# First attention of a four-layer network: weighing one unit later, six of eight norms inside its loop, and preparation of weights in single steps

## The chip, the cores and the metric

One core of one Trainium2 chip runs the kernel. Its engines are TensorE (PE, with the weight loads PEld shown apart), VectorE (DVE), ScalarE (ACT), GpSimd (POOL) and SyncE (SP, which here only issues DMAs). The metric is the time of one execution on the device in microseconds. The kernel before takes 2339.91 us, the median of three runs (2333.78 to 2342.82).

## The reference

Four layers in turn work on 8 sequences of 512 tokens with 128 features, all in float32. Each layer is a norm, an attention-like block, a gate, and a feed-forward block. The change touches the first attention, and weights that later layers use. What it computes on the normed input:

```python
def window_kv(t):
    pad = jnp.concatenate([jnp.zeros((B, H, W, hd), t.dtype), t], axis=2)
    prev = pad[:, :, :S].reshape(B, H, nb, W, hd)
    cur = t.reshape(B, H, nb, W, hd)
    return jnp.concatenate([prev, cur], axis=3)
kw = window_kv(k)
vw = window_kv(v)
scores = jnp.einsum('bhnqd,bhnkd->bhnqk', qb, kw) * scale
...
scores = jnp.where(valid, scores, NEG)
attn = jax.nn.softmax(scores, axis=-1)
out = jnp.einsum('bhnqk,bhnkd->bhnqd', attn, vw)
...
return out @ Wo.T + bo
```

with 16 heads of 8 features and windows of W = 64 tokens, each of which sees itself and the window before. The norm ahead of it is `(x - m) / sqrt(v + eps)` over the 128 features. The weights of the first feed-forward block come as integers and are decoded by `q / 7.5 - 1`, times a scale for each group of 16. The second layer mixes each token with the one before it, by weights per feature. The last layer needs some scalars per head (softplus and sigmoid of parameters).

## The kernel before, in words

`x` and `xn` (the normed input) lie in SBUF with features on the 128 partitions and all 4096 tokens along the row. A sequence ("batch" b) is one tile of 512 tokens.

**Order.** Most code calls the engines through a wrapper (`in_order`, L83), which keeps an engine's instructions in the order in which they are written; nearly every row of the profile therefore has line L83, and tile names tell the rows apart. What is called without the wrapper (constants, `l0_decode`, `l3_scalars`, loads) is placed by the scheduler where an engine's queue has room. The tile framework puts in all waits, also those for a buffer of a pool.

**Start** (`network`, L2781). SP issues eight loads of `x`, then those of the second and third layers' constants, then the first attention's weights `a0_w` (tile a_w) and `a0_b`, then the integers `f0_q` and their scales. `layer_norm` (L142) goes over all eight tiles: `centre` (four matmuls with the centring matrix, tile ps_c), `spread` (square on ACT, sum on DVE, power on POOL: sq, var, rstd), `scale` on DVE (row), `turn` (four transposes, ps_t), `keep` (copy to xn on ACT). `l0_decode` (L2691) turns the integers into weights on DVE. The constants of the third and second layers are filled; `fill` of the second layer (L738) issues the two big loads of the expert weights from ACT's queue and computes the mixing weights there (td, rest, wm). `l3_scalars` (L2730) is written behind the first layer but placed early by the scheduler.

**The attention** (`l0_attention`, L250) handles 64 units: unit u is half the heads of 128 tokens, eight units to a batch. `project` computes a batch's k, q and v in five steps; the first two write the four pieces of kb (the keys, masked by head group), alternately on DVE and ACT, out of one PSUM tile ps_k. `scores(u)` (PE: sc; DVE: scale and mask into e, then the row maximum mx; POOL: subtract) runs three units ahead, the exp on ACT two units ahead. `turned(u)` transposes the exponentials on PE (tp) and ACT copies them to SBUF (pt). `weigh(u)` multiplies them with the values (av). Every second unit closes a pair: `norm` divides on DVE (rec, o), `out_rows` transposes the result (tpo) and ACT adds the bias (ot). `finish` projects a batch out (ps_o). tp, tpo, ps_k, ps_q, ps_v, ps_o all take turns in one pool `p_t` of three PSUM buffers. The loop (L408) writes the parts of unit u in this order: `turned(u)`, `norm(u - 1)`, `scores(u + 3)`, `out_rows(u - 1)`, exp of u + 2, `weigh(u)`, `finish`, one step of `project`, and from the fifth batch on a step of `l0_low_rank`, which finishes the first feed-forward block's weights.

## Time and profile before

| what | value |
|---|---|
| median of three runs | 2339.91 us |
| the profiled execution: time, span | 2359.42 us, 2357.7 us |
| busy share of the span | PE 93%, DVE 85%, ACT 79%, POOL 67% |
| mean granted TensorE clock | 0.965 of full |
| first PE instruction of the attention (ps_k) | 29.09 us |
| first transposes of exponentials (tp) | 48.46 us |
| last output projection of the attention (ps_o) | from 311.94 us |

The profile is one execution. A row of the timeline has start, length, engine, line, operation, output and inputs, shape, count, and in brackets how long the engine had been idle before it and what ended that idle time. In the table of stretches each engine's busy time is followed by the number of its instructions, then come the granted clock, the share of time in which DMA engines were busy, and GB/s. A matmul in float32 shows as two passes, so four matmuls count x8; four transposes count x4.

### The profile page before, as it was taken

What the parts mean: (1) busy time and instruction counts of PE and PEld (TensorE: products, weight loads), DVE (VectorE), ACT (ScalarE), POOL (GpSimd) and SP (SyncE); (2) the same over time, 40 slices, a digit from 0 to 9 for tenths busy, and PEclk for the clock granted to TensorE, in tenths of its full rate; (3) what the DMA queues carried; (4) which work ended last, traced back from release to release, by engine and by line L of the source; (5) the groups of instructions that cost most, each with busy time, mean ns of one, the idle gap of its engine ahead of it and who ended that gap; (6) DMA issues with size and microseconds to landing.
All of it is one profiled execution on the core that took longest, in us unless ns stands there. A gap on an engine that the chain in (4) does not pass through costs nothing.

```text
span 2357.7 us, 48954 instructions
## 1 busy us (share of the span) xinstructions
PE 2186.5 (93%) x17762; PEld 1526.4 (65%) x17762; DVE 1996.3 (85%) x3579; ACT 1856.3 (79%) x3906; POOL 1576.9 (67%) x1414
## 2 busy tenths in 40 slices
PE   6999998899976999878999999999999999999888
PEld 4666676556523666645776777777777777777776
DVE  4777777985676999759999999999999999999656
ACT  4666664564533899848999999999999999999875
POOL 4444435355274788656788788887888878887554
PEclk7999988999997999989999999999999999999999
DMA  4000001013110000043443444334443344433100
GB/s 142 2 2 2 2 1 36 14 50 72 40 46 14 3 16 16 29 134 100 106 104 90 110 114 106 101 91 110 112 109 100 92 110 113 108 97 84 43 1 37
DMA packets 91617, 156.94 MB, mean 67 GB/s; under 512 B 20144, under 2 KB 44464, under 8 KB 91120
## 3 DMA queue, kind: packets, MB, share of 16 engines
q1 hardware_dynamic: 86736, 140.95, 22.9%
q0 software_dynamic: 4352, 8.92, 1.6%
q10 hardware_dynamic: 288, 3.93, 0.4%
q8 instruction: 142, 2.33, 0.4%
q14 instruction: 99, 0.81, 0.1%
HBM read 30.52 MB, written 12.06 MB: 18 GB/s over the span
## 4 chain that ended last, share of the span: by engine, by line
PE 56%; DVE 30%; issue 4%; ACT 4%; POOL 3%; DMA 1%; SPq 1%; another core or an unknown queue 0%; DVEq 0%; ACTq 0%; POOLq 0%
PE sc L83 10%; DVE sc L83 8%; DVE y L83 6%; DVE r L83 6%; PE ps_av L83 6%; PE ps_u L83 5%; PE tp L83 5%; PE ps_kq L83 4%; PE ps_ab L83 3%; PE av L83 3%; PE ps_n L83 2%; DVE mx L83 2%; DVE e L83 2%; PE ps_v L83 2%; PE ps_y L83 1%
## 5 line engine op out<-in xcount | busy, mean ns | idle before, releaser
L83 POOL TENSOR_TENSOR ek<-E,kn 128x512 f32<-128x512 f32 (+3 forms) x512 | 434.4, 871 | 206.3 <-DMA kn<-nr 205.1
L83 PE MATMUL sc<-r 128*128 128x512 f32 (+3 forms) x1024 | 310.2, 446 | 25.2 <-DVE y L83 22.2
L83 POOL TENSOR_TENSOR e<-e,mx 128x1024 f32<-128x1024 f32 x112 | 212.2, 1900 | 180.8 <-DVE mx L83 94.7
L83 POOL TENSOR_TENSOR r<-r,rs 128x1024 f32<-128x1024 f32 x128 | 304.4, 2378 | 23.0 <-DMA rs<-r 20.9
L83 PE MATMUL ps_av<-u,at 128*128 128x128 f32 x2560 | 307.9, 276 | 0.8 <-ACT o L83 0.8
L83 PEld LDWEIGHTS ps_av<-u,at 128*128 128x128 f32 x2560 | 297.3, 193 | 1.1 <-ACT o L83 1.1
L83 ACT ACTIVATE y<-y,mn 128x384 f32<-128x384 f32 (+3 forms) x512 | 288.6, 569 | 4.0 <-DVE mn L83 3.2
L83 PEld LDWEIGHTS sc<-r 128*128 128x128 f32 x1024 | 165.6, 192 | 190.0 <-issue 118.8
L83 DVE SCALAR_TENSOR_TENSOR y<-sc,qn,V 128x512 f32<-128x512 f32 (+3 forms) x512 | 246.5, 544 | 9.1 <-DVE sc L83 0.5
L83 DVE CUSTOM_DVE_ANT_0 y<-y,ps_g,ncs 128x384 f32<-128x384 f32 (+3 forms) x512 | 253.4, 541 | 0.0
L83 PEld LDWEIGHTS tp<-ident,y 128*128 128x128 f32 x1280 | 161.5, 141 | 115.3 <-issue 49.5
L83 ACT ACT_TABLE_LOAD x175 | 224.5, 1283 | 4.0 <-PEq L2879 0.8
L83 PE MATMUL tp<-ident,y 128*128 128x128 f32 x1280 | 203.9, 274 | 3.4 <-ACT o L83 1.4
L83 ACT COPY at<-tp 128x512 f32<-128x512 f32 (+1 forms) x384 | 195.2, 509 | 7.2 <-PE tp L83 4.4
L83 DVE TENSOR_TENSOR sc<-sc,EF 128x1280 f32<-128x1280 f32 x128 | 192.0, 1500 | 4.4
L83 DVE SCALAR_TENSOR_TENSOR sc<-sc,ek 128x1280 f32<-128x1280 f32 x128 | 189.8, 1483 | 6.5 <-issue 5.0
L83 POOL TENSOR_TENSOR s<-s,o 128x512 f32<-128x512 f32 x120 | 154.1, 1284 | 31.6 <-ACT o L83 31.6
L83 ACT ACTIVATE y<-y 128x1280 f32<-128x1280 f32 x128 | 163.4, 1277 | 5.1 <-DVE y L83 4.4
L83 DVE TENSOR_TENSOR r<-sn,ps_kq 128x1024 f32<-128x1024 f32 x128 | 155.3, 1213 | 9.6 <-ACT sq L83 5.1
L83 ACT ACTIVATE sq<-ps_kq 128x1024 f32<-128x1024 f32 x128 | 131.6, 1028 | 32.3 <-PE ps_kq L83 32.3
L83 DVE TENSOR_TENSOR r<-ct,ps_kq 128x1024 f32<-128x1024 f32 x128 | 155.3, 1213 | 0.0
L83 ACT ACTIVATE e<-e 128x1024 f32<-128x1024 f32 x112 | 117.3, 1062 | 40.9 <-POOL e L83 40.5
(465 smaller groups left out, 5023.3 us busy)
## 6 DMA issues: line engine op xcount, KB each, us to landing
rs<-r SPq DMA_DIRECT2D x256, 256.0 KB
kn<-nr SPq DMA_DIRECT2D x512, 64.0 KB
yrows<-yy SPq DMA_DIRECT2D x36, 128.0 KB
ct<-trig SPq DMA_DIRECT2D x16, 256.0 KB
EF<-E SPq DMA_DIRECT2D x16, 256.0 KB
EF<-E SPq DMA_DIRECT2D x16, 192.0 KB
m_w<-m_w ACTq DMA_DIRECT2D x1, 2560.0 KB
x<-x SPq DMA_DIRECT2D x8, 256.0 KB
```

What stands on the lines that cost most here:

```text
L83: ins = op(*args, **kwargs)
```

## The change

- **Norms.** `layer_norm` takes the number of tiles and does two. The other six are written into the attention's loop in five parts at fixed units: `centre` (PE to PSUM, copied to SBUF tile lc by ACT), `square` (ACT), `spread` (DVE sum, POOL power), `scale_rows` (four ACT scalings, where DVE had one multiply), `turn_rows` (PE transposes into p_t, ACT copy to xn). The norm of tile b has its centre in the last unit of batch b - 3 and its turn in unit 6 of batch b - 2; tile 2 is done within batch 0.
- **Weighing.** `weigh(u - 1)` stands where `weigh(u)` stood. `norm`, `out_rows` and `finish` are a unit later; a pair closes in odd units. pt moves to the pool with four buffers. The loop has one iteration more.
- **Preparation in steps.** `l0_decode`, the mixing weights and `l3_scalars` are generators, called in order at three units of each batch from the second on. The multiply with the scales moves from DVE to POOL; the load of the last layer's parameters is issued by SP behind all others.
- **Loads.** The second and third layers' constants are loaded behind the first layer's. The expert weights are loaded from SP's queue instead of ACT's.

The core of the diff:

```diff
-    def layer_norm(self, x, xn, gamma=None, beta=None, banks=(5, 3), free=False):
+    def layer_norm(self, x, xn, gamma=None, beta=None, banks=(5, 3), free=False, n=NTB):
...
-                pt = p3.tile([P, 4, P], F32, tag="pt", name="pt")
+                pt = p5.tile([P, 4, P], F32, tag="pt", name="pt")
...
+        mid, sqs, std = {}, {}, {}
+        def centre(b):
+            ps = p_t.tile([P, 4, P], F32, tag="t", name="ps_c")
+            for k in range(4):
+                pe.matmul(
+                    ps[:, k, :], lhsT=x[:, ts(4 * b + k, P)], rhs=net.cmat,
+                    start=True, stop=True,
+                )
+            mid[b] = p2.tile([P, 4, P], F32, tag="lc", name="lc")
+            act.copy(mid[b], ps)
+        def square(b):
+            sqs[b] = p2.tile([P, 4, P], F32, tag="sq", name="sq")
+            act.activation(sqs[b], mid[b], AF.Square, scale=net.inv_root)
+        def spread(b):
+            var = p2.tile([P, 4], F32, tag="var", name="var")
+            std[b] = p2.tile([P, 4], F32, tag="rstd", name="rstd")
+            dve.tensor_reduce(var, sqs.pop(b), AX.X, ALU.add)
+            dve.tensor_scalar(var, var, EPS, None, ALU.add)
+            pool.tensor_tensor(std[b], var, net.neg_half.to_broadcast([P, 4]), ALU.pow)
+        def scale_rows(b):
+            for k in range(4):
+                act.activation(
+                    mid[b][:, k, :], mid[b][:, k, :], AF.Copy, scale=std[b][:, k : k + 1]
+                )
+        def turn_rows(b):
+            ps = p_t.tile([P, 4, P], F32, tag="t", name="ps_t")
+            for k in range(4):
+                pe.transpose(ps[:, k, :], mid[b][:, k, :], net.ident)
+            act.copy(xn[:, ts(b, S)], ps.rearrange("p k q -> p (k q)"))
+        norms = {}
+        for b in range(2, B):
+            c = U * (b - 3) + 7 if b > 2 else 1
+            for part, at in (
+                (centre, c), (square, c + 1), (spread, c + 2), (scale_rows, c + 4),
+                (turn_rows, U * (b - 2) + 6),
+            ):
+                norms.setdefault(at, []).append((part, b))
+        def early():
+            yield from net.prep.l0_decode(dve, pool)
+            yield from l1.mixing(act)
+            yield from net.prep.l3_scalars(dve, act)
+        rest = early()
         todo = iter(())
-        for u in range(N + 2):
+        pts = {}
+        for u in range(N + 3):
...
-            ended = u >= 1 and u <= N and u % 2 == 0
+            ended = u >= 3 and u % 2 == 1
             if u < N:
-                pts = turned(u)
+                pts[u] = turned(u)
             if ended:
-                o = norm(u - 1)
+                o = norm(u - 2)
...
-            if u < N:
-                weigh(u, pts)
-            if u >= U and u % U == 1:
+            if 1 <= u <= N:
+                weigh(u - 1, pts.pop(u - 1))
+            if u >= U and u % U == 2:
                 finish(u // U - 1)
             next(todo, None)
+            for part, b in norms.get(u, ()):
+                part(b)
+            if u >= U and u % U in (1, 3, 6):
+                next(rest, None)
...
-            if u > 4 * U and u % U == 6:
+            if u > 4 * U and u % U == 5:
                 next(low, None)
...
-        self.w13 = net.load(p1, "m1_w13", act)
-        self.w2 = net.load(p1, "m1_w2", act)
+        self.w13 = net.load(p1, "m1_w13")
+        self.w2 = net.load(p1, "m1_w2")
...
-    def l0_decode(self):
-        nc, wt, qw, sc = self.net.nc, self.f0_wt, self.qw, self.sc
-        nc.vector.tensor_copy(wt, qw)
-        nc.vector.tensor_scalar(wt, wt, 1.0 / 7.5, -1.0, ALU.mult, ALU.add)
-        nc.vector.tensor_tensor(wt, wt, sc, ALU.mult)
+    def l0_decode(self, dve, pool):
+        wt, qw, sc = self.f0_wt, self.qw, self.sc
+        dve.tensor_copy(wt, qw)
+        yield
+        dve.tensor_scalar(wt, wt, 1.0 / 7.5, -1.0, ALU.mult, ALU.add)
+        yield
+        pool.tensor_tensor(wt, wt, sc, ALU.mult)
+        yield
...
-            net.layer_norm(x, xn)
-            prep.l0_decode()
+            l2.load()
+            l1.load()
+            net.layer_norm(x, xn, n=2)
             l2.fill()
             l1.fill()
-            l0_attention(net, xn, s, p0, w0, b0)
+            l0_attention(net, x, xn, s, p0, w0, b0, l1)
             l0_ffn(net, x, xn, s, l1)
-        prep.l3_scalars()
```

`l1.mixing` holds the instructions that computed td, rest, wm in `fill`, and `l3_scalars` the same instructions as before, both with a `yield` every few of them. The step of `l3_scalars` with the function Ln stands alone.

More of the change, by code (lines that the diff above doesn't have):

```diff
@@ L190, in keep @@
                     act.activation(xn[:, ts(t, TB)], ps, AF.Identity, scale=gamma, bias=beta)
-            for t in range(NTB + 3):
-                if t < NTB:
+            for t in range(n + 3):
+                if t < n:
                     centre(t)
                     spread(t)
-                if 2 <= t < NTB + 2:
+                if 2 <= t < n + 2:
                     scale(t - 2)
@@ L247, in window_mask, with l0_attention @@
             )
-def l0_attention(net, xn, s_out, p0, w, bias):
+def l0_attention(net, x, xn, s_out, p0, w, bias, l1):
     nc, tc = net.nc, net.tc
@@ L418, in l0_attention @@
             if ended:
-                out_rows(u - 1, o)
+                out_rows(u - 2, o)
             if u + 2 < N:
                 act.activation(e[u + 2], e[u + 2], AF.Exp)
-            if u < N:
-                weigh(u, pts)
-            if u >= U and u % U == 1:
+            if 1 <= u <= N:
+                weigh(u - 1, pts.pop(u - 1))
+            if u >= U and u % U == 2:
                 finish(u // U - 1)
             next(todo, None)
+            for part, b in norms.get(u, ()):
+                part(b)
+            if u >= U and u % U in (1, 3, 6):
+                next(rest, None)
             if u == 4 * U:
@@ L430, in l0_attention @@
                 )
-            if u > 4 * U and u % U == 6:
+            if u > 4 * U and u % U == 5:
                 next(low, None)
+        for _ in rest:
+            pass
 L0_FFN = (
@@ L729, in __init__, with load @@
         self.net = net
-        self.p1 = p1 = st.enter_context(tc.tile_pool(name="a1_c", bufs=1))
+        self.p1 = st.enter_context(tc.tile_pool(name="a1_c", bufs=1))
+    def load(self):
+        net, nc, p1, E = self.net, self.net.nc, self.p1, self.E
         self.rw = net.load(p1, "m1_r")
@@ L739, in fill @@
         net, nc, p1, E = self.net, self.net.nc, self.p1, self.E
-        act = net.in_order(nc.scalar)
-        self.w13 = net.load(p1, "m1_w13", act)
-        self.w2 = net.load(p1, "m1_w2", act)
-        w, par = self.w, self.par
-        self.td = td = p1.tile([P, 1], F32, tag="td", name="td")
-        act.activation(td, par[:, 0:1], AF.Exp)
-        act.activation(td, td, AF.Copy, scale=-1.0)
-        self.tf = par[:, 1:2]
-        self.wm = wm = p1.tile([P, 3, 2, P], F32, tag="wm", name="wm")
-        self.rest = rest = p1.tile([P, 3], F32, tag="rest", name="rest")
-        act.activation(rest, par[:, 2:5], AF.Identity, scale=-1.0, bias=net.ones[:, 0:1])
-        for i in range(3):
-            act.activation(wm[:, i, 0, :], w[:, i, :], AF.Copy, scale=par[:, 2 + i : 3 + i])
-            act.activation(wm[:, i, 1, :], w[:, i, :], AF.Copy, scale=rest[:, i : i + 1])
-        act.activation(w[:, 3, :], w[:, 3, :], AF.Copy, scale=0.5)
+        self.w13 = net.load(p1, "m1_w13")
+        self.w2 = net.load(p1, "m1_w2")
         def counting(tag, shape, pattern, base=0, channel=0):
@@ L778, in fill, with mixing @@
         nc.gpsimd.memset(self.keep[:, :, 0:1], 0.0)
+    def mixing(self, act):
+        net, p1, w, par = self.net, self.p1, self.w, self.par
+        self.td = td = p1.tile([P, 1], F32, tag="td", name="td")
+        act.activation(td, par[:, 0:1], AF.Exp)
+        act.activation(td, td, AF.Copy, scale=-1.0)
+        yield
+        self.tf = par[:, 1:2]
+        self.wm = wm = p1.tile([P, 3, 2, P], F32, tag="wm", name="wm")
+        self.rest = rest = p1.tile([P, 3], F32, tag="rest", name="rest")
+        act.activation(rest, par[:, 2:5], AF.Identity, scale=-1.0, bias=net.ones[:, 0:1])
+        yield
+        for i in range(3):
+            act.activation(wm[:, i, 0, :], w[:, i, :], AF.Copy, scale=par[:, 2 + i : 3 + i])
+            act.activation(wm[:, i, 1, :], w[:, i, :], AF.Copy, scale=rest[:, i : i + 1])
+            yield
+        act.activation(w[:, 3, :], w[:, 3, :], AF.Copy, scale=0.5)
+        yield
 def l1_layer(net, x, xn, s_out, consts, l2):
@@ L1344, in __init__, with load @@
         self.net = net
-        self.p1 = p1 = st.enter_context(tc.tile_pool(name="a2_c", bufs=1))
+        self.p1 = st.enter_context(tc.tile_pool(name="a2_c", bufs=1))
+    def load(self):
+        net, p1 = self.net, self.p1
         self.w = net.load(p1, "a2_w")
@@ L2689, in l0_load @@
         self.f0_wt = p1.tile([P, 6, P], F32, tag="wt", name="wt")
-    def l0_decode(self):
-        nc, wt, qw, sc = self.net.nc, self.f0_wt, self.qw, self.sc
-        nc.vector.tensor_copy(wt, qw)
-        nc.vector.tensor_scalar(wt, wt, 1.0 / 7.5, -1.0, ALU.mult, ALU.add)
-        nc.vector.tensor_tensor(wt, wt, sc, ALU.mult)
+    def l0_decode(self, dve, pool):
+        wt, qw, sc = self.f0_wt, self.qw, self.sc
+        dve.tensor_copy(wt, qw)
+        yield
+        dve.tensor_scalar(wt, wt, 1.0 / 7.5, -1.0, ALU.mult, ALU.add)
+        yield
+        pool.tensor_tensor(wt, wt, sc, ALU.mult)
+        yield
     def l0_low_rank(self, p1, bank, pe, dve, act):
@@ L2728, in l0_low_rank, with l3_scalars @@
             yield
-    def l3_scalars(self):
+    def l3_scalars(self, dve, act):
         net, nc, p1 = self.net, self.net.nc, self.p1
@@ L2739, in l3_scalars @@
         raw = par[:, 1:5, :]
-        nc.vector.scalar_tensor_tensor(sp, raw, -1.0, raw, ALU.mult, ALU.min)
-        nc.scalar.activation(sp, sp, AF.Exp)
-        nc.scalar.activation(sp, sp, AF.Ln, bias=net.ones[:, 0:1])
-        nc.vector.scalar_tensor_tensor(sp, raw, 0.0, sp, ALU.max, ALU.add)
-        sig2, eta2, gam2, nu = (sp[:, i, :] for i in range(4))
         def vec(tag):
@@ L2749, in l3_scalars @@
         mu, nmu, v_e2, v_0, coef = vec("mu"), vec("nmu"), vec("v_e2"), vec("v_0"), vec("coef")
-        nc.scalar.activation(mu, par[:, 0, :], AF.Exp, scale=-1.0)
-        nc.vector.tensor_scalar(mu, mu, 1.0, None, ALU.add)
-        nc.vector.reciprocal(mu, mu)
-        nc.vector.tensor_scalar(mu, mu, 1e-4, None, ALU.add)
-        nc.vector.tensor_scalar(nmu, mu, -1.0, None, ALU.mult)
-        nc.vector.tensor_scalar(v_e2, nmu, 2.0, None, ALU.mult)
-        nc.vector.reciprocal(v_e2, v_e2)
-        nc.vector.tensor_tensor(v_e2, v_e2, sig2, ALU.mult)
@@ L2759, in l3_scalars @@
-        nc.vector.tensor_tensor(v_0, eta2, gam2, ALU.add)
-        nc.vector.tensor_tensor(v_0, v_0, v_e2, ALU.subtract)
-        nc.vector.tensor_scalar(coef, nu, float(DH), -0.5, ALU.add, ALU.mult)
-        nc.vector.tensor_tensor(coef, coef, par[:, 5, :], ALU.mult)
+        yield
+        dve.scalar_tensor_tensor(sp, raw, -1.0, raw, ALU.mult, ALU.min)
+        act.activation(sp, sp, AF.Exp)
+        act.activation(mu, par[:, 0, :], AF.Exp, scale=-1.0)
+        yield
+        act.activation(sp, sp, AF.Ln, bias=net.ones[:, 0:1])
@@ new lines, in l3_scalars @@
+        yield
+        dve.scalar_tensor_tensor(sp, raw, 0.0, sp, ALU.max, ALU.add)
+        sig2, eta2, gam2, nu = (sp[:, i, :] for i in range(4))
+        yield
+        dve.tensor_scalar(mu, mu, 1.0, None, ALU.add)
+        dve.reciprocal(mu, mu)
+        dve.tensor_scalar(mu, mu, 1e-4, None, ALU.add)
+        dve.tensor_scalar(nmu, mu, -1.0, None, ALU.mult)
+        dve.tensor_scalar(v_e2, nmu, 2.0, None, ALU.mult)
+        dve.reciprocal(v_e2, v_e2)
+        dve.tensor_tensor(v_e2, v_e2, sig2, ALU.mult)
@@ L2765, in l3_scalars @@
+        yield
+        dve.tensor_tensor(v_0, eta2, gam2, ALU.add)
+        dve.tensor_tensor(v_0, v_0, v_e2, ALU.subtract)
+        dve.tensor_scalar(coef, nu, float(DH), -0.5, ALU.add, ALU.mult)
+        dve.tensor_tensor(coef, coef, par[:, 5, :], ALU.mult)
+        yield
         norm_0 = vec("norm_0")
-        nc.vector.tensor_tensor(norm_0[0:64], nu[0:64], v_e2[0:64], ALU.mult)
-        nc.vector.tensor_tensor(norm_0[64:128], nu[64:128], v_0[64:128], ALU.mult)
+        dve.tensor_tensor(norm_0[0:64], nu[0:64], v_e2[0:64], ALU.mult)
@@ L2768, in l3_scalars @@
+        dve.tensor_tensor(norm_0[64:128], nu[64:128], v_0[64:128], ALU.mult)
         cs, ncs, inv_cs, g_v = vec("cs"), vec("ncs"), vec("inv_cs"), vec("g_v")
-        nc.vector.scalar_tensor_tensor(cs, coef, -1.0, coef, ALU.mult, ALU.max)
-        nc.vector.tensor_scalar(cs, cs, 1e-18, 2e-18, ALU.is_lt, ALU.mult)
-        nc.vector.tensor_tensor(cs, cs, coef, ALU.add)
-        nc.vector.tensor_scalar(ncs, cs, -1.0, None, ALU.mult)
-        nc.vector.reciprocal(inv_cs, cs)
-        nc.vector.tensor_scalar(g_v, coef, -1.0, -0.5 * DH, ALU.mult, ALU.add)
@@ L2777, in l3_scalars @@
-        nc.vector.tensor_tensor(g_v, g_v, inv_cs, ALU.mult)
+        yield
+        dve.scalar_tensor_tensor(cs, coef, -1.0, coef, ALU.mult, ALU.max)
+        dve.tensor_scalar(cs, cs, 1e-18, 2e-18, ALU.is_lt, ALU.mult)
+        dve.tensor_tensor(cs, cs, coef, ALU.add)
+        dve.tensor_scalar(ncs, cs, -1.0, None, ALU.mult)
+        dve.reciprocal(inv_cs, cs)
+        dve.tensor_scalar(g_v, coef, -1.0, -0.5 * DH, ALU.mult, ALU.add)
+        dve.tensor_tensor(g_v, g_v, inv_cs, ALU.mult)
         self.scalars = nu, nmu, v_e2, v_0, norm_0, ncs, inv_cs, g_v
+        yield
```

## The prediction

> **What bounds the kernel now.** I read the table of stretches first, then the timeline of the start, the waits inside the attention, and TensorE's own timeline in one batch. The whole change lies in the first 314 us of a span of 2357.7 us, so nothing behind that is costed except where it is named.

> The stretches are cut where a batch's key projection starts. Columns: stretch, length, busy time of PE, PEld, DVE, ACT and POOL, granted clock, DMA share, GB/s.

> ```profile
> 0.00:28.46 28.46, 18.04 (x96) 16.69 (x96) 13.43 (x28) 10.17 (x17) 17.08 (x62) 0.88 0.55 156
> 28.46:48.46 20.00, 8.45 (x42) 3.71 (x42) 10.90 (x31) 10.32 (x22) 6.78 (x13) 0.71 0.50 198
> 48.46:88.59 40.13, 38.30 (x455) 25.34 (x455) 25.78 (x30) 22.84 (x36) 18.22 (x10) 0.85 0.01 1
> 120.43:152.28 31.85, 30.51 (x410) 19.97 (x409) 23.56 (x28) 20.80 (x33) 15.18 (x9) 1.00 0.01 2
> 299.64:314.00 14.36, 13.12 (x121) 10.79 (x122) 2.25 (x8) 4.48 (x8) 1.46 (x1) 0.50 0.01 2
> ```

> In a steady batch (eight units) PE is busy 30.5 of 31.85 us, no other engine above 23.6. So PE sets the pace of the attention and has 1.34 us to spare per batch. In the first 48.46 us no engine is near its limit: that is a chain of latencies. The last row is PE busy at half clock.

> The timeline of the start shows what the chain waits for:

> ```profile
> 10.88 4.00 POOL L83 TENSOR_TENSOR rstd<-var,neg_half 128x4 f32<-128x4 f32 x4
> ...
> 30.26 0.81 DVE L83 TENSOR_SCALAR kb<-ps_k,hm,kbias 128x512 f32<-128x512 f32 x1 [1.50 <-PE ps_k L83]
> ...
> 34.50 0.76 ACT L83 ACTIVATE kb<-ps_k,kbias,hm 128x512 f32<-128x512 f32 x1
> 35.27 1.28 ACT L2742 ACT_TABLE_LOAD   x1
> 35.29 0.81 DVE L83 TENSOR_SCALAR kb<-ps_k,hm,kbias 128x512 f32<-128x512 f32 x1 [3.22 <-ACT kb L83]
> ...
> 38.35 0.76 ACT L83 ACTIVATE kb<-ps_k,kbias,hm 128x512 f32<-128x512 f32 x1
> ```

> The four pieces of kb take turns on DVE and ACT, 3.14 us of work, yet last from 30.26 to 39.11: ACT does the mixing weights (32.55 to 34.50) and two table loads of the last layer's scalars in between.

> In the attention itself, with what PE waited for in brackets:

> ```profile
> 155.53 1.13 PE L83 MATMUL av<-vw,pt 128*64 128x9 f32 x32 [0.30 <-ACT pt L83]
> ...
> 158.62 0.66 PE L83 MATMUL tp<-ident,e 128*128 128x128 f32 x4 [0.48 <-DVE s L83]
> ...
> 176.09 0.30 PE L83 MATMUL tpo<-ident,o 128*128 128x128 f32 x1 [0.25 <-DVE o L83]
> ```

> These, with a second tpo wait of the same size, make up the 1.34 us. The waits also list "PEld av <- ACT pt", 30.1 us in 40 times, which looks like the prize of weighing later. It is not: the weight load starts about 0.8 us late behind every scores matmul, and behind scores tpo shows the same delay under another name (PEld tpo <- PE sc, 14.3 us in 13 times, 1.1 each).

> **The change, part by part.**

> *Two norms instead of eight ahead of the attention, and the loads of w0 first.* POOL's 49 constants ahead of rstd stay, so rstd still starts at 10.88, 1.00 each: std of tile 1 at 12.9, its row (0.69) at 13.6, its four transposes (0.87) at 14.5. The projection follows at once: ps_k 1.13 to 15.6. With mixing weights and scalars gone from ACT, the two DMA issues (2.09 us of ACT's queue) now on SP, kb takes its bare 3.14 plus four handovers of 0.05: end at 18.9 instead of 39.11. From there the order is the old one: the second half of ps_v waits for the PSUM buffer that ps_k gives back (39.16 before), scores start 1.6 later (40.74), the first transposes 7.7 later (48.46). So everything moves by 20.2; I take **-20.0**. Covers: masks and vw on POOL took 28.53 to 33.26, that is 4.7, from 14.5 to 19.3 now, and are needed at 22.6 (scores plus 2.1); without that cover 1 us per us late. w0 is needed at 14.5; it is now issued ninth, about 4.6. Before, f_q issued at 13.55 was waited for until 18.40, that is 4.9; twice that is 14.3, so I cost it at nothing and keep 3 us as the bad end. Behind it on SP come f_q, the scales, the L2 and L1 weights, the 3.75 MB of experts, then par: the first needed is f_q by unit 9 (some 50 us later), par at unit 35. Bounds -17 to -21.

> *Six norms inside.* Each adds four matmuls ps_c and four transposes ps_t to PE. At full clock the norm of before shows 1.17 (23.04, eight passes) and 0.63 (24.70); back to back the tails overlap by 0.1 each: 1.6. So PE needs 30.5 + 1.6 = 32.1 per batch, already 0.3 over the old period. ACT gets a copy 0.59, a square 0.60, four scalings 1.2, a copy 0.59 (rows of 128x512 and 128x128 above): 20.8 + 3.0 = 23.8. DVE +0.86, POOL +1.0. No engine passes PE.

> *Where a stall goes.* The rows go out in odd units now (tpo in 1, 3, 5, 7), and each even unit has a projection or ps_t behind its weighing, so DVE has o ready: the two waits of 0.25 go. The wait on pt goes too, since av is a unit late. But unit 1 of a batch gains a tpo where p_t's three buffers hold ps_k and the two fresh tp. It waits until pt is copied, and ACT has kb and now square ahead of that copy. From the start of unit 0's transposes: scores end at 2.1, e and mx until 4.65, kb on DVE 5.45, kb on ACT 6.25, square 6.85, pt 7.4; PE stood ready at 6.1. That is **1.3 to 1.4 idle**, where before 0.30 + 0.48 were lost. I find no other wait above 0.2 in the walk through the eight units, since ACT has pt, exp and at most two copies per unit of 4 us. A batch with a norm becomes 32.1 + 1.4 = 33.5, +1.6. Five such warm batches: **+8**. Bounds per batch: +0.3 (no idle) to +3 (idle as before and the new one).

> *First batch.* ps_c and ps_t at half clock 1.92 + 1.06 = 3.0, against 1.83 idle in 40.13: 1.2 to 3.0, taken **+2**. *Batches 6 and 7*, without a norm: 1.6 idle in 216.60 to 249.40 becomes about 1.1: **-1** for both.

> *Scalars and mixing weights as steps.* Six scalings at 0.3, 0.4 each are in units with ACT slack. The step with Ln brings the table loads, 1.28 twice plus 0.35, into unit 38, on top of pt, exp and xn (2.7): 5.6 against 4 us of PE. The exp is two units ahead, so what is late next is pt, then p_t's buffers: 0 to 2.6, taken **+1**. Decoding on DVE is 0.56 and 0.55. The multiply with the scales on POOL: nearest row 128x1024 in 1.90, so 1.4; queued behind it is the subtraction for a unit whose exp is later; POOL is busy 15.2 of 31.85. Cover gone, it would cost its 1.4 once: 0 to 1.4, taken 0. rstd (1.01) waits in the same queue for var, which is there some 3 us ahead of the next mx: 0.

> *The tail.* One av (1.88 at half clock) and one tpo move from the steady part (1.03 and 0.26) into the last, cold stretch: **+1** (0 to 2).

> Sum: -20 + 8 + 2 - 1 + 1 + 1 = **-9**. The profiled execution took 2359.42 around its span of 2357.7, 0.8% above the median of the three runs, 2339.91. The difference is taken over as it stands: **2331**.

> *The clock.* Row first: from 299.64 to 314.00 PE is busy 13.12 of 14.36 and gets 0.50, with nothing but tp, av and tpo; and once in the steady part, from 258.9 to 262.3, it falls to 0.50 although PE worked 5.15 of the 6 us before. [...] My sum goes by the row: one such fall in seven batches, and it stays in.

> **The rivals.** A measurement of this kernel can tell about 0.5% from no change, that is 11.7 us: faster is below 2328.2, slower above 2351.6.

> 1. *The loop gives nothing back.* If p_t's buffers come free in time, the 1.34 idle per batch pays for most of the norm: 5 x 0.3, and 1 or 2 for batch 0 and the tail: -17, **2323**. For it: PE's spare time is there in every batch. Against it: kb's chain (ACT kb <- DVE kb, 25.2 us) is untouched and a tpo stands behind it now.
> 2. *Cold windows, one in each batch.* The one of before made ps_q 2.08 and tp 1.74 where 1.12 and 1.04 are usual: 1.66 lost. Seven of them: 11.6, **2343**, no change to be told.
> 3. *The slower side: PE's clock falls twice a batch.* Place: units 0 to 2, at the wait for p_t, and units 5 to 7. From 13 windows on (-9 + 13 x 1.66 = 12.6) it decides; two in each of seven batches cost 23: **2354**. For it: the cold tail shows that this mix has little to spare. Against it: the batches between 88.59 and 249.40 all ran at 1.00 with 1.3 idle each.

> That the start doesn't shrink (w0 late, or the order of issue) is the bad end of its bound, 3 us, and lies inside the first case.

> **How the numbers follow.** My case 0.54 (2324 to 2337: bounds of start, batches and table load taken together; 0.20 of it below 2328.2); rival 1 0.22; rival 2 0.12; rival 3 0.12. Faster 0.20 + 0.22 = 0.42, same 0.34 + 0.12 = 0.46, slower 0.12. The range leaves out half of rival 3, the far side of it and the best of rival 1: 2317 to 2347.

> **What would show it.** First transposes tp at 28 to 29 instead of 48.46; if above 32, w0 or the masks were late. From one ps_k to the next 33 to 34 us in the second to sixth batch, with an idle of more than 1 us ahead of tpo in the unit behind ps_k, ended by ACT pt; 32 and no such wait is rival 1. A granted clock below 1.00 in several batches is rival 2 or 3. No PE wait on pt ahead of av. A time under 2317 would mean that PE's sequence got shorter than its own instructions here; one over 2350 with the clock at 1.00 would mean a wait that I have not seen.

## The result, and the profile after

The changed kernel takes 2370.14 us (median of four runs, 2364.67 to 2374.53) against 2341.3 us of the kernel before on the same chip: a ratio of 1.0124, 95% interval 1.0092 to 1.0156. It is 29 us slower; the forecast was 9 us faster.

The profiled execution took 2374.53 us around a span of 2372.8, 15.1 us more than before's. The granted clock of the whole span is 0.945 (0.965 before). The page shows the place: in its 40 slices (59 us each) the first six have a low clock, and PE is busy there nonetheless.

```profile
PE   7999999889997999868999999999999999999888
...
PEclk7888759899997999978999999999999999999999
```

The table of stretches of the changed kernel, the second and third row cut again where a key projection starts, the last two at 291 us, where the clock falls, and at the tail (columns as before: stretch, length, busy PE, PEld, DVE, ACT, POOL, granted clock, DMA share, GB/s):

```profile
0.00:28.94 28.94, 14.65 (x66) 9.47 (x67) 11.22 (x16) 7.79 (x11) 17.87 (x69) 0.81 0.73 239
28.94:70.25 41.31, 39.60 (x441) 25.95 (x441) 26.75 (x29) 26.05 (x44) 19.31 (x11) 0.84 0.09 37
107.89:145.53 37.64, 36.36 (x425) 23.81 (x421) 24.90 (x30) 24.59 (x46) 16.17 (x9) 0.86 0.01 1
291.20:332.41 41.21, 39.95 (x351) 25.34 (x351) 22.38 (x28) 17.68 (x27) 13.74 (x8) 0.58 0.00 1
332.41:346.85 14.44, 13.20 (x152) 11.69 (x152) 2.24 (x8) 4.56 (x9) 1.43 (x1) 0.50 0.01 2
```

The first row is the part that came out as forecast: tp starts at 28.94 instead of 48.46, 19.5 us earlier. All of that and more is lost behind it. The first instructions of the key projections and of the last output projection give this balance, in us (the forecast's terms are shared out to the stretches in which they fall):

| stretch | before | after | difference | forecast |
|---|---|---|---|---|
| to the first tp | 48.46 | 28.94 | -19.5 | -20 |
| first tp to unit 8 | 40.06 | 41.31 | +1.2 | +2 |
| units 8 to 39, four batches | 128.10 | 151.25 | +23.2 | +7.4 |
| units 40 to 47 | 32.78 | 46.40 | +13.6 | about +1 |
| unit 48 to the last ps_o | 62.54 | 78.95 | +16.4 | about +0.5 |

The rows add up to +34.9 us, in an execution of the changed kernel that was 4.4 us above its median.

Behind the attention both kernels issue the same 14386 PE instructions. That stretch took 2025.95 us after and 2045.76 before, at a clock of 0.97 in both. No part of the change acts there, and before's profiled execution was 18 us above its median. The experiments below ran in three groups on three chips, and the kernel before took 2341, 2343 and 2365 us there. In the traces of the first two groups the stretch behind the attention takes 2016 to 2025 us, in those of the third 2039 to 2053, at about the same clock. So the 20 us may well be the difference between two chips; on which chip before's profile was taken is not known.

PE did not stand idle more. From the first tp to the last ps_o it was busy 250.89 of 263.48 us before and 305.69 of 317.91 after. The groups of PE's instructions in that stretch (shape, count, busy us, mean ns, idle before and what ended it) say what grew. Before:

```profile
L83 PE MATMUL av<-vw,pt 128*64 128x9 f32 x2048 | 74.3, 208 | 3.1 <-ACT pt L83 2.5
L83 PE MATMUL tp<-ident,e 128*128 128x128 f32 x512 | 73.8, 288 | 5.2 <-DVE s L83 2.9 <-ACT e L83 2.3
L83 PE MATMUL sc<-kb,q 32*64 32x512 f32 x488 | 67.2, 620 | 0.0
```

After:

```profile
L83 PE MATMUL tp<-ident,e 128*128 128x128 f32 x512 | 87.0, 324 | 5.6 <-ACT e L83 3.2 <-ACT kb L83 1.7 <-ACT q L83 0.7
L83 PE MATMUL av<-vw,pt 128*64 128x9 f32 x2048 | 85.2, 220 | 0.0
L83 PE MATMUL sc<-kb,q 32*64 32x512 f32 x488 | 80.2, 732 | 0.0
...
L83 PE MATMUL ps_c<-cmat,x 128*128 128x128 f32 x48 | 6.9, 288 | 0.0
L83 PE MATMUL ps_t<-ident,lc 128*128 128x128 f32 x24 | 4.4, 311 | 0.0
```

The counts are the same and each instruction is longer. These three groups grew by 37.1 us, ps_o, ps_q, ps_k and tpo by 10; the six norms are 11.3. So of the 54.4 us by which this stretch grew, some 47 are PE's clock, on instructions that were there before.

Where it falls is seen in the timeline of PE at the second unit of a batch (start, length, instruction, and in brackets the idle time before it and what ended it):

```profile
72.18 1.09 PE L83 MATMUL sc<-kb,q 32*64 32x512 f32 x8
74.56 0.33 PE L83 MATMUL tpo<-ident,o 128*128 128x128 f32 x1 [1.29 <-ACT pt L83]
74.81 1.10 PE L83 MATMUL av<-vw,pt 128*64 128x9 f32 x32
75.85 1.73 PE L83 MATMUL tp<-ident,e 128*128 128x128 f32 x8
77.51 1.98 PE L83 MATMUL sc<-kb,q 32*64 32x512 f32 x8
```

The 1.29 us ahead of tpo is the wait that the forecast has, in its place and size. Then tp takes 1.73 where it has 1.04 elsewhere, and sc 1.98 for 1.09. The stretches of half clock in the attention are, in us: before 48.5 to 57, 64 to 68, 259 to 262, 300 to the end; after 29 to 35, 42 to 49, 76 to 86, 114 to 124, 151 to 161, 189 to 199, 226 to 237, 250 to 271, 291 to 325, 332 to the end. Between the first tp and the last ps_o these are 28 us before and 134 after. In each of the 13 traces that were cut into windows (all but that of the second experiment) the clock in the attention changes only on a grid of 3.413 us, so it can be read in windows of that length. After, on its grid:

```profile
69.32:72.73 3.41, 3.41 (x50) 2.35 (x50) 3.20 (x4) 1.06 (x1) 1.02 (x2) 1.00 0.01 2
72.73:76.15 3.42, 2.13 (x44) 1.45 (x37) 3.06 (x5) 3.42 (x6) 1.34 (x2) 1.00 0.00 0
76.15:79.56 3.41, 3.41 (x19) 1.47 (x18) 2.32 (x4) 2.78 (x5) 3.12 (x2) 0.50 0.00 0
79.56:82.97 3.41, 3.41 (x34) 2.49 (x35) 2.44 (x2) 0.00 (x0) 0.69 (x1) 0.50 0.02 5
82.97:86.39 3.42, 3.42 (x10) 1.81 (x9) 1.21 (x3) 1.11 (x2) 1.21 (x1) 0.50 0.00 0
86.39:89.80 3.41, 3.41 (x51) 2.29 (x50) 1.89 (x2) 2.06 (x4) 0.00 (x0) 1.00 0.00 0
```

The window that holds the wait (PE busy 2.13) still has the full clock; the next three have half, although PE is busy in every microsecond of them. The five falls at 76.1, 113.7, 151.2, 188.8 and 226.3 are 11 windows (37.55 us) apart. A batch takes 37.64 us, so each batch meets the grid at nearly the same place and falls again.

### The profile page after: what moved, and what is told of

Same layout as the page of the kernel before. It is cut to its first block, busy times and chain, and to the rows that moved or that the text cites. A ratio compares the mean times of both kernels' runs of the same rounds, so it can differ in the third digit from the quotient of the medians.

```text
span 2372.8 us, 48943 instructions
## 1 busy us (share of the span) xinstructions
PE 2228.0 (94%) x17762; PEld 1551.5 (65%) x17762; DVE 2001.2 (84%) x3572; ACT 1864.8 (79%) x3936; POOL 1578.5 (67%) x1415
## 3 DMA queue, kind: packets, MB, share of 16 engines
q8 instruction: 142, 2.33, 0.4%
## 4 chain that ended last, share of the span: by engine, by line
PE 60%; DVE 25%; POOL 6%; ACT 4%; issue 3%; DMA 2%; SPq 1%; POOLq 0%; ACTq 0%; DVEq 0%
PE sc L83 11%; DVE sc L83 7%; DVE y L83 6%; DVE r L83 6%; PE tp L83 6%; PE ps_av L83 5%; PE ps_u L83 4%; PE ps_kq L83 4%; PE av L83 4%; PE ps_ab L83 3%; PE ps_n L83 2%; PE ps_v L83 2%; PE ps_y L83 1%; PE ps_p L83 1%; POOL yr L83 1%
## 5 line engine op out<-in xcount | busy, mean ns | idle before, releaser
L83 POOL TENSOR_TENSOR ek<-E,kn 128x512 f32<-128x512 f32 (+3 forms) x512 | 433.4, 868 | 210.3 <-DMA kn<-nr 206.1
L83 POOL TENSOR_TENSOR e<-e,mx 128x1024 f32<-128x1024 f32 x112 | 212.2, 1900 | 217.4 <-DVE mx L83 141.3
L83 PE MATMUL sc<-r 128*128 128x512 f32 (+3 forms) x1024 | 311.1, 447 | 26.3 <-DVE y L83 23.5
L83 POOL TENSOR_TENSOR r<-r,rs 128x1024 f32<-128x1024 f32 x128 | 303.9, 2374 | 22.3 <-DMA rs<-r 21.0
L83 PE MATMUL ps_av<-u,at 128*128 128x128 f32 x2560 | 307.8, 276 | 0.8 <-ACT o L83 0.8
L83 PEld LDWEIGHTS ps_av<-u,at 128*128 128x128 f32 x2560 | 297.1, 193 | 1.1 <-ACT o L83 1.1
L83 ACT ACTIVATE y<-y,mn 128x384 f32<-128x384 f32 (+3 forms) x512 | 288.4, 569 | 4.0 <-DVE mn L83 3.2
L83 PEld LDWEIGHTS sc<-r 128*128 128x128 f32 x1024 | 166.0, 192 | 191.7 <-issue 121.8
L83 DVE SCALAR_TENSOR_TENSOR y<-sc,qn,V 128x512 f32<-128x512 f32 (+3 forms) x512 | 246.6, 544 | 8.8
L83 DVE CUSTOM_DVE_ANT_0 y<-y,ps_g,ncs 128x384 f32<-128x384 f32 (+3 forms) x512 | 253.2, 540 | 0.0
L83 PEld LDWEIGHTS tp<-ident,y 128*128 128x128 f32 x1280 | 161.5, 141 | 115.5 <-issue 49.5
L83 PE MATMUL tp<-ident,y 128*128 128x128 f32 x1280 | 203.9, 274 | 3.4 <-ACT o L83 1.4
L83 ACT COPY at<-tp 128x512 f32<-128x512 f32 (+1 forms) x384 | 195.0, 508 | 7.5 <-PE tp L83 4.5
L83 DVE SCALAR_TENSOR_TENSOR sc<-sc,ek 128x1280 f32<-128x1280 f32 x128 | 189.7, 1482 | 9.2 <-issue 6.0
L83 DVE TENSOR_TENSOR sc<-sc,EF 128x1280 f32<-128x1280 f32 x128 | 191.9, 1499 | 4.4
L83 POOL TENSOR_TENSOR s<-s,o 128x512 f32<-128x512 f32 x120 | 153.7, 1281 | 33.1 <-ACT o L83 33.1
L83 ACT ACTIVATE y<-y 128x1280 f32<-128x1280 f32 x128 | 163.4, 1277 | 6.7 <-DVE y L83 6.0
L83 DVE TENSOR_TENSOR r<-sn,ps_kq 128x1024 f32<-128x1024 f32 x128 | 155.2, 1212 | 10.4 <-ACT sq L83 5.4
L83 ACT ACTIVATE sq<-ps_kq 128x1024 f32<-128x1024 f32 x128 | 131.5, 1027 | 33.5 <-PE ps_kq L83 33.5
L83 DVE TENSOR_TENSOR r<-ct,ps_kq 128x1024 f32<-128x1024 f32 x128 | 155.1, 1211 | 0.0
L83 DVE SCALAR_TENSOR_TENSOR e<-sc,maskFalse 128x1024 f32<-128x1024 f32 (+1 forms) x96 | 90.4, 952 | 75.9 <-PE sc L83 71.3
```

The lines of the kernel that those rows point to most:

```text
L83: ins = op(*args, **kwargs)
```

## The experiments

### Added work in the second unit

Is it the clock, and not the wait itself or a part of the start? Three matmuls that nothing reads fill the wait:

```diff
...
+            if u >= U and u % U == 1 and u < N - U:
+                for _ in range(3):
+                    pe.matmul(spare, lhsT=net.cmat, rhs=x[:, 0:224], start=True, stop=True)
             if ended:
                 out_rows(u - 2, o)
```

(`spare` is the unused end of the PSUM bank of av.)

> The changed kernel with three more matmuls (128x224, into unused columns of av's bank, read by nobody) ahead of tpo in unit 1 of the second to seventh batch, where TensorE waits 1.3 us for a buffer of p_t. They need about 1.2 us. Theory A (the clock falls because TensorE's array gets too little dense work around that wait): the falls behind unit 1 go, some 10 us at half clock each, so the kernel gets FASTER by added work, by 20 to 30 us, to 2340 to 2350; the falls near ps_l and in the last batches stay. Theory B (the clock has nothing to do with that place, for example a fall each 37 us whatever runs): the falls stay, time 2370 to 2378. Theory C (the wait itself costs, not the clock): time 2365 to 2375.

Measured: 2337.93 us (2329.96 to 2347.71), ratio to before 0.9988, 0.9965 to 1.0011. Work was added, and the kernel is some 32 us faster than without it. The falls at 76 to 226 us are gone; half clock is left at 28 to 35, 233 to 243 and 291 to 311. The window with the second unit, and the one behind it:

```profile
69.10:72.51 3.41, 3.41 (x48) 2.23 (x40) 3.05 (x6) 3.14 (x6) 1.58 (x1) 1.00 0.00 0
72.51:75.93 3.42, 3.42 (x51) 2.35 (x50) 3.39 (x6) 2.95 (x5) 3.07 (x2) 1.00 0.02 5
```

The 512 tp, 2048 av and 488 sc take 73.6, 75.0 and 68.1 us of PE, about as in the kernel before. The clock costs nearly the whole of the loss.

### The row transpose without the wait for a buffer

```diff
...
-            tp = p_t.tile([P, 4, P], F32, tag="t", name="tpo")
-            pe.transpose(tp[:, 0, :], o...
+            tp = bank[:, 288:416]
+            pe.transpose(tp, o...
...
```

> The changed kernel with tpo written into unused columns of av's bank instead of a buffer of p_t, so that tpo waits for no buffer in unit 1. Theory A1 (the idle 1.3 us makes the clock fall): no fall behind unit 1 in the second to sixth batch, time 2335 to 2350. Theory A2 (it is the distance between dense matmuls, idle or not: scores of one unit to those of the next with ps_o gone from between): the gap shrinks from 3.6 to 2.3 us and some falls stay, time 2350 to 2362. Theory B: as before, 2365 to 2372, less about 6.

Measured: 2420.51 us, ratio 1.0329 (1.0298 to 1.0361). This missed its purpose: tpo now shares a bank with av, and av waits for ACT's copy of tpo (0.46 us in most pairs, 1.7 to 1.8 in the second unit of a batch). It removes one wait and makes another; the granted clock of the profiled span is 0.935 (0.945 in the changed kernel), and behind the waits of 1.7 to 1.8 us (86.6, 127.7 and 168.7 us) the weighing takes 1.88 us instead of 1.11. It says only that here longer waits came with less clock.

### Undoing the later weighing, and undoing the norms inside

```diff
-            ended = u >= 3 and u % 2 == 1
+            ended = u >= 1 and u <= N and u % 2 == 0
...
-                o = norm(u - 2)
+                o = norm(u - 1)
...
-                weigh(u - 1, pts.pop(u - 1))
+                weigh(u, pts.pop(u))
...
```

(`out_rows`, `finish`, the steps of `l0_low_rank` and the number of iterations go back with it.)

> The changed kernel with the old order in the loop: weigh(u) in unit u, pairs closed in even units, finish in unit 1, low rank in unit 6; six norms inside, steps and later loads stay. Theory A: ps_o stands in unit 1 again and tpo isn't queued behind ps_k's buffer, so the clock stays near 1.00 as before: 2341 - 20 for the start + 8 to 10 for the norms, 2326 to 2336. Rival N (the norms' transposes and copies make the clock fall): falls stay, time 2350 to 2370.

Measured: 2368.44 us, ratio 1.0093 (1.0064 to 1.0121). No gain that can be told: av now waits 1.02 us for pt in the same unit, because the square of the norm stands ahead of pt on ACT, and half clock between the first tp and the last ps_o is still 99 us.

```diff
-            net.layer_norm(x, xn, n=2)
+            net.layer_norm(x, xn)
...
-        for b in range(2, B):
+        for b in ():
```

> The changed kernel with all eight norms ahead of the attention again and none in the loop; weighing one unit later, steps and later loads stay. Theory A: the wait in unit 1 shrinks to about 0.8 (no square ahead of pt), but ps_o is still away from unit 1: some falls stay; start about 10 us later than in the changed kernel: 2350 to 2372. Rival N: no falls, 2325 to 2335.

Measured: 2355.59 us, ratio 1.0062 (1.0036 to 1.0089). Without the square the wait ahead of tpo is 0.77 us, and of five it leads to a fall once (142 us); two more falls (187 and 221 us) follow a wait of 0.34 us for q a unit or two behind it. The last batches lose the clock as in the changed kernel (232 to 252, 273 to 307 and 314 to 334 us). First tp is at 38.2: loads and steps alone bring 10 us of the start.

### The row transpose behind the weighing

```diff
-            if ended:
+            if ended and u % U != 1:
                 out_rows(u - 2, o)
...
                 weigh(u - 1, pts.pop(u - 1))
+            if ended and u % U == 1:
+                out_rows(u - 2, o)
```

> The changed kernel with one edit and no added work: in the second unit of each batch the row transpose tpo stands behind the 32 weighing matmuls instead of ahead of them, so that PE weighs (1.03 us) while ACT copies pt. Theory A (idle time in a window of 3.41 us decides the clock; 1.28 us of it costs some 10 us at half clock): the idle ahead of tpo falls to about 0.3 us, the five falls at 76, 114, 151, 189 and 226 us go, time 2336 to 2345 as with the added matmuls (2338). Rival A2 (what counts is how many dense matmuls are in the window, and the added ones helped by being dense): the second unit still has none, the falls stay, 2362 to 2372. Rival D (the wait's own time is what costs): 5 x 1 us, 2365.

Measured: 2362.09 us, ratio 1.0074 (1.0053 to 1.0096): theory A's 2336 to 2345 is a miss. The wait did not shrink to 0.3, it was spread: 0.21 ahead of tpo, 0.16 and 0.56 ahead of the two tp behind it. More telling is the window before the fall at 145.6 us: PE was busy 3.06 of 3.41 us, so only 0.35 us of idle time were in it. The kernel before has windows with more idle time behind which the full clock stays (busy 2.64 of 3.42 us at 91.5, 2.86 of 3.41 at 125.7). Idle time alone doesn't order them. The windows of this run and of the kernel before:

```profile
142.13:145.55 3.42, 3.06 (x47) 1.78 (x45) 3.06 (x5) 2.78 (x5) 1.90 (x1) 1.00 0.00 0
145.55:148.96 3.41, 2.90 (x14) 1.02 (x12) 2.50 (x4) 2.90 (x8) 2.63 (x2) 0.50 0.01 2
```

```profile
125.67:129.08 3.41, 2.86 (x28) 1.42 (x28) 2.79 (x6) 1.60 (x3) 1.90 (x1) 1.00 0.00 0
129.08:132.49 3.41, 3.41 (x46) 2.17 (x44) 1.88 (x2) 2.84 (x6) 1.26 (x1) 1.00 0.02 5
```

### What kind of work keeps the clock

In place of the three matmuls, nine transposes:

```diff
-                for _ in range(3):
-                    pe.matmul(spare, lhsT=net.cmat, rhs=x[:, 0:224], start=True, stop=True)
+                for _ in range(9):
+                    pe.transpose(spare[:, 0:P], x[:, 0:P], net.ident)
```

> As the run with three added matmuls ahead of tpo in the second unit (2337.93), but with nine transposes of 128x128 in their place, about 1.4 us of PE at full clock. Theory A (idle decides while the clock is full): the falls at 76 to 226 us go, 2336 to 2348. Rival A2 (transposes count as idle): falls as in the changed kernel and 5 x 0.3 us more of PE, 2365 to 2375.

Measured: 2340.08 us, ratio 0.9976 (0.9955 to 0.9997). All five falls are gone; the last batches still have half clock (237 to 247, 268 to 302, 309 to 329 us). PE's timeline of this run and the window (first two columns: window, length; then busy PE):

```profile
73.27 1.20 PE L83 MATMUL av<-ident,x 128*128 128x128 f32 x9
74.58 0.33 PE L83 MATMUL tpo<-ident,o 128*128 128x128 f32 x1
74.84 1.10 PE L83 MATMUL av<-vw,pt 128*64 128x9 f32 x32
75.88 1.09 PE L83 MATMUL tp<-ident,e 128*128 128x128 f32 x8
```

```profile
73.21:76.63 3.42, 3.30 (x53) 2.87 (x50) 3.10 (x4) 3.05 (x6) 1.34 (x2) 1.00 0.00 0
76.63:80.04 3.41, 3.41 (x47) 1.93 (x45) 3.27 (x6) 2.69 (x4) 2.67 (x2) 1.00 0.03 5
```

Then narrow matmuls of the weighing's shape, in place of the transposes:

```diff
...
+                for _ in range(22):
+                    pe.matmul(
+                        spare[0:W, 0:9], lhsT=net.cmat[:, 0:W], rhs=x[:, 0:9],
+                        start=True, stop=True,
+                    )
```

> As the run with three added matmuls ahead of tpo (2337.93) and the one with nine added transposes (2340.08), but with 22 matmuls of the shape of the weighing (64 columns of weights, 9 columns streamed), about 1.4 us. PE is then as little idle in the second unit as in those two runs. Theory A (idle time decides): no falls at 76 to 226 us, 2336 to 2346. Theory W, formed from the windows of all runs so far (what decides is how much work of the full array is in a window of 3.41 us: transposes and matmuls of 128 columns or more count in full, the scores of 32 rows about half, the weighing nothing): four or five of the five falls stay, 2362 to 2378.

Measured: 2392.41 us beside 2365.05 of before in this group of runs, ratio 1.0116 (1.0089 to 1.0142). This group ran on the third chip, so only its ratios can be compared with those of the other groups; the changed kernel, which wasn't run in it, has 1.0124. The added work took 2.73 us, not the 1.4 assumed, so part of the time is its own. The verdict rests on the windows, not on the time:

```profile
72.31 2.73 PE L83 MATMUL av<-x,cmat 128*64 128x9 f32 x44
74.97 0.33 PE L83 MATMUL tpo<-ident,o 128*128 128x128 f32 x1
75.23 1.86 PE L83 MATMUL av<-vw,pt 128*64 128x9 f32 x32
```

```profile
71.87:75.29 3.42, 3.42 (x55) 2.84 (x49) 3.06 (x5) 2.19 (x4) 1.34 (x2) 1.00 0.00 0
75.29:78.70 3.41, 3.41 (x41) 3.27 (x40) 2.25 (x4) 2.46 (x4) 3.04 (x2) 0.50 0.02 5
```

PE is busy in all of the window from 71.87 to 75.29, and the clock falls at its end, as it does in all five batches (75, 116, 154, 195, 232). This speaks against idle time as the profile shows it, and for theory W: too little work of the wide kind lets the clock fall. It leaves a rival open. Each of the 44 records is 0.20 us long and they start 0.06 us apart, so together they fill the stretch, though each streams only nine columns. The profile's busy time doesn't tell how much of that the array works, so it may be the streaming itself that counts, with the weights below as a rough measure of it. Nor do these runs separate the nine columns from the 64 columns of weights.

To see how far that goes I split the windows of seven profiled executions (before, after, and the five runs that undo or move a part: the two of weighing and norms, the late row, and two below; one of these two has wide matmuls added in its last three units, taken as sc) by tile and looked for weights. In the fit, the next window has the full clock when

```
0.31 sc + 0.64 (tp, tpo, ps_t) + 0.73 (ps_k, ps_q, ps_v, ps_o, ps_c) + 0.15 (ps_l, ps_b) + 0 av  >  1
```

where each term is the tile's busy time in the window in us, halved in a window at half clock. The fit is worked out from these windows alone. It is right in 560 of 572 windows; PE's busy time alone, halved in the same way and with its best threshold, in 490; the guess that the clock stays as it is, in 469. With the weight of the transposes at 0, and again the best threshold, it is 497. Of the 103 changes of the clock the fit gets 91. The same weights on three later runs (the narrow matmuls, and two runs below) are right in 237 of 244. Some windows, worked out:

```
kernel       window   PE busy   sum of the fit    next window
before       122.25   3.12      1.09              full
before       125.67   2.86      1.48              full
after         72.73   2.13      0.57              half
late row     142.13   3.06      0.95              half
3 matmuls     69.10   3.41      1.49              full
9 transposes  73.21   3.30      1.48              full
22 narrow     71.87   3.42      0.35              half
after, at half clock:
              76.15   3.41      0.76              half
              79.56   3.41      0.63              half (ps_o 1.73, av 1.75)
              82.97   3.42      1.33              full (tp 1.57, ps_q and ps_o 2.26)
```

Two things follow from the fit. The weighing, a third of a unit's time, counts nothing in it, so a unit without a projection is just above 1 at full clock (windows of sc 1.09, tp 1.09, av 1.44 give 1.03 and hold). And at half clock the same units do about half as much per window (sc takes 1.98 us there instead of 1.09), and the sum is below 1 (0.76 at 76.15): in the changed kernel the clock returned with ps_o and ps_q in the next unit (in the last batches with ps_k at 268 and ps_o at 320 us), or, where no projection follows, as in the tail, not before the attention ended.

### The preparation steps

> The parts that remain when both the woven norms and the later weighing are undone: the loop of before, eight norms ahead, preparation of weights in steps, loads later. If these gain at the start what the run with all norms ahead showed (first transposes tp at 38.2 instead of 48.5 us) and the loop keeps the clock as before (some 42 us at half clock): 2341 - 10 = 2331 (2325 to 2338). Rival: the steps put small VectorE operations ahead of the row's division and so idle time into the loop, which costs windows: one or more falls between 100 and 290 us beside the one at 258, 2341 to 2352.

This run has both of the edits that undo a part: before's loop, with steps and later loads alone. Measured: 2366.46 us, ratio 1.0087 (1.0069 to 1.0104); the rival's direction, and beyond its range. Half clock between the first tp and the last ps_o is 87 us, and PE waits up to 2.25 us ahead of tpo for the row o. The cause stands in the timelines of the changed kernel too, where a step of the last layer's scalars comes just ahead of the division of a row. VectorE, GpSimd and PE there:

```profile
241.88 0.17 DVE L83 TENSOR_SCALAR mu<-mu 128x16 f32<-128x16 f32 x1
242.08 0.25 DVE L83 RECIPROCAL mu<-mu 128x16 f32<-128x16 f32 x1
242.37 1.69 DVE L83 TENSOR_SCALAR mu<-mu 128x16 f32<-128x16 f32 x1
```

```profile
242.13 1.90 POOL L83 TENSOR_TENSOR e<-e,mx 128x1024 f32<-128x1024 f32 x1 [5.89 <-DVE mu L83]
```

```profile
248.06 0.30 PE L83 MATMUL tpo<-ident,o 128*128 128x128 f32 x1 [0.65 <-DVE o L83]
```

An operation of 0.17 us takes 1.69 and ends (244.06) with GpSimd's subtraction (244.03). The row comes 0.65 us late, ps_l with its 32 rows counts little, and the clock falls at 250.2 for 20 us. Then the same run with the scalars behind the attention:

```diff
-            if u >= U and u % U in (1, 3, 6):
+            if U <= u < 4 * U and u % U in (1, 3, 6):
                 next(rest, None)
```

> The run e7 (start only, 2366.46) with one edit: the steps of the last layer's scalars stand behind the attention instead of in batches 5 to 8; decoding and mixing weights stay in the loop. If the scalars cause that run's loss, by VectorE's small operations ahead of the row's division (waits of 2.25 us ahead of tpo at 242 us) and the table load at 208 us, the falls at 211, 242 and 262 us go: 2366 - 0.5 x (24 + 7 + 3) - 6 of idle = 2343 (2332 to 2348). Rival (the later loads, or the start's shift against the windows, cause it): 2358 to 2368.

Measured: 2365.79 us beside 2365.05 of before in its group, ratio 1.0009 (0.9986 to 1.0031), which is 2343 where before takes 2341. The falls at 211 and 242 us are gone, half clock between the first tp and the last ps_o is 44 us: the scalars inside the loop cost that run 0.8%. The 10 us of its start are still not seen in the time. In its trace the first batches have half clock at 38 to 46, 53 to 67, 125 to 128 and 159 to 162; before's has the first two (48 to 57, 64 to 68) but not the last two. Those come right behind waits that before doesn't have, and ACT has a step of the mixing weights (td, wm) ahead of pt there, which this run keeps in the loop:

```profile
123.60 1.13 PE L83 MATMUL av<-vw,pt 128*64 128x9 f32 x32 [0.40 <-ACT pt L83]
...
157.89 1.13 PE L83 MATMUL av<-vw,pt 128*64 128x9 f32 x32 [0.65 <-ACT pt L83]
```

So the other steps seem to cost windows too. That the batches begin elsewhere on the grid may also play a part; neither was tried by itself.

### Removing the low windows together

> The changed kernel with three edits: tpo behind the weighing in the second unit; the last layer's scalars only at units 1 and 3 of a batch, not 6, so that VectorE has the row o ready for the seventh unit; and in the last three units, where no scores are left, two 512-wide matmuls into a free PSUM tile that nothing reads. Theory A: half clock is left only at the start (28 to 35 us) and at most one stretch elsewhere; of the run with added matmuls (2338, 35 us at half clock) the stretches 233 to 244 and 291 to 311 go, which is half of 31 us less 3 us of added work: 2322 to 2330. Rival (the last stretches have another cause than idle time): they stay, 2336 to 2342.

The edits are the late row, scalars at units 1 and 3 alone, and in the last three units

```diff
+            elif u < N:
+                warm = p_sc.tile([P, 8, 2 * W], F32, tag="sc", name="sc")
+                for i in range(2):
+                    pe.matmul(
+                        warm[:, 4 * i : 4 * i + 4, :], lhsT=net.ident, rhs=q[B - 1],
+                        start=True, stop=True,
+                    )
```

Measured: 2349.53 us, ratio 1.0037 (1.0021 to 1.0053), outside both ranges. The stretches at the end went as expected (291 to 311 is 307 to 311), but the second unit, with the late row, lost the clock in three batches (116, 184 and 222 us), and it fell once behind it (89). With the three matmuls in place of the late row:

> The changed kernel with the three added matmuls of the first experiment, the last layer's scalars only at units 1 and 3, and two 512-wide matmuls in each of the last three units. Theories A and W both: the windows of the second unit, of the seventh (2.33 us of idle at 230 us) and of the last units are lifted; half clock is left at the start and in at most one short stretch: 2337.93 - 0.5 x (10 + 20) + 3 = 2326 (2320 to 2333). Rival (the time moves to another wait): 2334 to 2340.

Measured: 2357.39 us beside 2365.05, ratio 0.9962 (0.9934 to 0.9989), which is 2332 where before takes 2341. Behind the start, half clock in the attention is left at 42 to 50 and 292 to 295 us; the attention from first tp to last ps_o has a clock of 0.97:

```profile
28.70:304.80 276.10, 266.90 (x3359) 179.99 (x3360) 202.00 (x257) 184.35 (x316) 126.96 (x70) 0.97 0.02 7
```

This version is faster than the kernel before by 7.7 us of 2365, 0.4%, with work added that nothing uses; the changed kernel is 1.2% slower than before in its own group. Last, the same tail in the kernel before:

> The kernel before with two 512-wide matmuls, into a PSUM tile that nothing reads, in each of the last three units, where no scores are left. Theories A and W: the fall at 300 us goes; 17 us at half clock cost 8.5, the added work 3: about -5, 2337 (2332 to 2341), ratio 0.996 to 1.000. Rival (the fall there has another cause): +3, ratio 1.001 or more.

Measured: 2365.41 us beside 2365.05, ratio 0.9991 (0.9975 to 1.0006). The fall at 300 us is gone from the trace, but the gain is too small to be told from none. This one trace has other falls (66 to 80 and 168 to 172 us), and with them as much half clock between the first tp and the last ps_o as before's, 29 us against 28. So what the tail alone is worth isn't shown.

## Why the prediction was wrong

*The start* (-20): right, -19.5, in part by luck. ps_k took 2.07 us at half clock instead of 1.13, so kb ended at 20.95 and not at 18.9; the first scores, 1.11 us at full clock where before took 2.01, won back part of it. Masks and loads were hidden as worked out.

*No wait on pt ahead of av*: right, 2.5 us before and 0.0 after. *The wait in unit 1* (1.3 to 1.4): right, 1.28 to 1.29. *Six norms*: 11.3 us of PE against 9.6. *The step with Ln* (+1): nothing; PE has no wait on ACT from 207 to 222 us, though the table loads are there (215.03 and 217.92). That depends on the unit: in two runs where the step stands elsewhere, PE waited 1.00 us (before's loop with the steps, at 209.7 us) and 1.76 us (the fastest version, at 217.1 us) behind the same loads. *The loop as a whole*: forecast +11. With the falls of the second unit taken away by three matmuls it is 276.6 us against 263.5, +13, with about as much half clock as before (31 us against 28). So the sum of instructions and waits was about right, once the clock is out of it.

*What failed is the step on the clock*: "My sum goes by the row: one such fall in seven batches, and it stays in." It put the cost of the clock at nothing more than before's; measured are 134 us at half clock in the attention instead of 28, some 47 us of PE's time. Two readings behind it were off: PE worked 5.45, not 5.15, of the 6 us before the fall at 258.9, and the stretch from 299.64 also holds a ps_l and the last ps_o. Three things in the step were wrong.

- How often. One fall in seven batches was carried over, and the batches at 1.00 stood against more of them, as if 1.3 us of idle time per batch were harmless. But most of before's idle time (1.0 of the 1.3 us) lies in units with a projection: ps_k, ps_o and ps_q are in units 0, 1 and 2. The change moved `finish` to unit 2, so that unit 1 has the longest wait and no projection at all. The forecast treated the wait as time lost, not as a place.
- What each costs. Rival 2 took 1.66 us from a fall of one window that ps_q ended at once. Each of the five falls lasts three windows, 10.24 us: a batch takes 37.6 us against the forecast 33.5, and 33.3 in the run with three matmuls, so a little over 4 us each. The trace of before had this price in view: 14 us at half clock at its end, with no projection until the last ps_o.
- *The tail* (+1) and *batches 6 and 7* (-1): measured +13.6 for units 40 to 47 and +16.4 from unit 48 on, where the forecast comes to about +1 and +0.5. The step took them for short of stalls. Their units hold the scalars and ps_l, and from the norms only one ps_t, so they have the fewest wide matmuls; one fall of 0.65 us of idle time lasts 20 us, one at 291 us lasts 34.

Rival 3 has the right sign and the right places (the wait for p_t, units 5 to 7). It has two short falls in a batch where there was one long one, and with 2354 too few microseconds, for the same reason as rival 2. PE's busy time does not tell where a fall comes: the window ahead of one had PE busy 2.13 us, and with narrow matmuls all of its 3.42 us, while nine transposes in the same place kept the clock in five batches out of five.

Not settled: whether a changed kernel without added work can keep the clock. The late row didn't; moving the square off ACT's queue ahead of pt, or a projection into the second unit, wasn't tried. Open too is what in a narrow matmul makes it count so little.

## What to carry to other kernels

When PE sets the pace, add up by window what the array does in wide matmuls and transposes, and look for the unit that has the least; a wait that is moved into that unit can cost several times its length (here 1.3 us of wait and a little over 4 us of clock). Where the units behind it are light, price a fall by the time until the next projection, not by one window (here 10.24 us in a batch, 34 us from 291). A few wide instructions into unused PSUM, in the lightest unit, test this in one run (here three matmuls, and all five falls were gone).
